# New fronts of the state space layer, and where the fp8 attention rounds its first inputs

## The chip, the cores and the metric

The kernel runs on one core of one Trainium2 chip. A core has five engines that work side by side: TensorE (PE, matrix products into PSUM; its weight loads are counted apart as PEld), VectorE (DVE), ScalarE (ACT), GpSimd (POOL) and SyncE (SP, which here only issues DMAs). Each engine takes its own instructions in order and waits at semaphores for the others. The metric is the device time of one execution in microseconds (us), lower is better.

## The reference

The program is a decoder of four layers with three blocks each, on x of 4 batches x 256 tokens x 256 channels. Every block adds its output to x; all but the last take a layer norm of x as input. The change concerns the tenth block, a state space layer (L3_attn), and its seams with the ninth (a mixture of 8 experts, L2_ffn) and the eleventh (attention with fp8 inputs, L3_xattn).

The state space layer, with 512 inner channels, 16 states and a dt rank of 128:

```python
def _L3_attn_ref(x, W_in, conv_w, conv_b, W_x, W_dt, b_dt, A_log, D, W_out):
    xz = x @ W_in
    xp, z = jnp.split(xz, 2, axis=-1)
    xc = lax.conv_general_dilated(jnp.transpose(xp, (0, 2, 1)), conv_w, (1,), [(1, 1)], feature_group_count=d, ...)
    xc = jax.nn.silu(jnp.transpose(xc + conv_b[None, :, None], (0, 2, 1)))
    x_dbl = xc @ W_x
    dt_in, Bm, Cm = x_dbl[..., :R], x_dbl[..., R:R + S], x_dbl[..., R + S:]
    dt = jax.nn.softplus(dt_in @ W_dt + b_dt)
    A = -jnp.exp(A_log)
    def step(h, ins):
        u_t, dt_t, B_t, C_t = ins
        h = jnp.exp(dt_t[:, :, None] * A) * h + dt_t[:, :, None] * B_t[:, None, :] * u_t[:, :, None]
        return (h, jnp.einsum('bds,bs->bd', h, C_t))
    xsT = (jnp.swapaxes(xc, 0, 1), jnp.swapaxes(dt, 0, 1), jnp.swapaxes(Bm, 0, 1), jnp.swapaxes(Cm, 0, 1))
    _, yT = lax.scan(step, h0, xsT)
    y = (jnp.swapaxes(yT, 0, 1) + xc * D) * jax.nn.silu(z)
    return y @ W_out
```

The convolution runs along the tokens, three taps per channel, one token to each side. The attention behind it normalises x with weights, divides it by four different scales per channel (for q, qx, k and v), and rounds each of the four to bf16 and then to fp8 (e4m3fn) before the products with the weights:

```python
def _div_clamp_fp8(x, scale):
    y = jnp.clip(x.astype(jnp.float32) / scale, -FP8_MAX, FP8_MAX)
    y = y.astype(jnp.bfloat16).astype(jnp.float32)
    return _fp8_roundtrip(y)
```

## The kernel before

x stays in SBUF as 8 tiles of 128 tokens; `k.XNT` holds the normed rows transposed, channels on the partitions. The blocks follow each other; a block's code may also carry pieces of the next one (generators, advanced with `next`), and these pieces are then in the queues among the block's own instructions.

**The mixture of experts** (`l2_ffn`, L1364) leaves the order of its instructions to a scheduler. It loads the state space layer's weights (`l3_loads`, L1415) and carries `l3_ahead` (L1436) in its second half: it multiplies the taps into three copies of the convolution's half of W_in (three DVE products, L1443, with the taps broadcast by three DMAs), norms and turns batches 0 and 1, and computes the front of batch 0.

**A front** (`l3_front`, L1450) is what a batch needs before its scan. PE computes the convolved xp in four tiles of 128 channels with six matmuls each (L1461 to L1465: for the middle tap whole, for the outer taps shifted by a token, two halves of the 256 input channels each), and ACT adds the bias (L1466). PE computes z (L1473), ACT copies it (L1474) and takes the Silu of both (L1476, L1477). PE multiplies by W_x in two banks, one for dt's 128 rows (L1481) and one for B and C (L1486), with an ACT copy each (L1483, L1488); B and C go to DRAM (`bcd`), from where they come back broadcast over the partitions (`bcb`, L83). PE multiplies by W_dt (L1500), and softplus is put together from Abs and Relu (L1504, L1505), Exp (L1507), two DVE operations (L1508, L1509), Ln (L1511) and two POOL operations (L1512, L1514); a third POOL operation, L1516, gives dt times xc (`du`).

**The scan** (`l3_attn`, L1520) has 64 steps g: per batch four chunks c of 128 channels, and in each four groups q of four states. In a step ACT computes the decays of step g+1 into PSUM (`decays`, L1552 four times, L1553), POOL the inputs of step g+2 (`inputs`, L1560), DVE scans step g along the tokens into PSUM (`scan`, L1567, 128 x 1024) and multiplies by C (L1569); PE adds the states of step g-1 up in PSUM with four products by the identity (`sums`, L1579). After each fourth step DVE adds xc times D (`close`, L1586) and POOL multiplies by the Silu of z (L1587). The order on PE, ACT, DVE and POOL is the order of the code here; SP's is scheduled. Tiles come from pools: `unit` has six buffers for inputs and products, `da` two, `h` one, `mm` (the PSUM bank of fronts, turns and outputs) one, `bcb` nine.

Into the steps of batch b are put: one piece per step of the front of batch b+1 (from step 0); from step 10 the norm and turn of batch b+2; at steps 1 and 2 the two output products of batch b-1 with W_out (L1592), each with its addition to x on DVE (L224) right behind; in batches 0 to 2 from step 3 the preparation of the attention's weights (`prepared`: means with ACT, DVE L1854 and L1855, POOL L1857; small scales on DVE, L1872 to L1896; splits into three bf16 parts, ACT L1868 and POOL L1869); in batch 3 from step 4 the norm and turn of the next block's first three batches (`Rows`, L1904; L1928 and L1931 on DVE, L1941 on ACT).

**The fp8 attention** (`l3_xattn`, L1945) starts, in order, with four times scaling (ACT, two products per input, L1988) and rounding (`rounded`, L1990: ACT Abs, then DVE L261, L262, L263, L264) for batch 0, then the scaling for batch 1, then the products of pass 0 (a pass is one batch with one group of heads; 16 passes). The first pass's vectors are normed in two halves: ACT squares (L2043), DVE reduces (L2045) and takes an inverse root by small integer and float steps (L2054 to L2056 and L120 to L129), POOL multiplies (L2059). The rounding of batch 1 is put between them, one input behind each part. Then come turns, scores (PE L2085) with their maximum on DVE (L407), and so on. `early` puts work for later passes into the first ones, among it the scaling and rounding of batches 2 and 3. The routing of the twelfth block (`Routing`, L1664) uses the rounded inputs' memory in passes 14 and 15.

Of the kernel before, what the change touches and what calls it, by code (L numbers as in the profile page):

```python
# [24 lines left out]
P = 128  # L25
# [1389 lines left out]
def l3_loads(k):  # L1415
    nc, a, v = k.nc, k.a, k.nc.vector
    s, s2 = k.wslot(), k.wslot()
    m = k.ssm = {}
    m["win"], m["wx"], m["wdt"] = s.take(2, 1024), s.take(4, 160), s.take(512)
    m["wout"], m["taps"] = s2.take(4, 256), [s2.take(2, 512), s2.take(2, 512)]  # L1420
    k.load(m["win"], rows(a["L3_attn_W_in"]))
    m["soft"] = lambda: k.t([P, 4, S], F32, "soft", 2, k.st)
    soft = [m["soft"]().rearrange("p c t -> p (c t)") for _ in range(2)]
    m["tap"] = [soft[0][:, :512], soft[0][:, 512:], soft[1][:, :512]]
    for i in range(3):
        k.load(m["tap"][i], a["L3_attn_conv_rows"][i : i + 1, :].rearrange("o m -> (o m)").partition_broadcast(P))
    k.load(m["wx"], rows(a["L3_attn_W_x"]))
    k.load(m["wdt"], a["L3_attn_W_dt"])
    k.load(m["wout"], rows(a["L3_attn_W_out"]))
    m["na"] = na = k.t([P, 64], F32, "na", 1, k.st)  # L1430
    nc.scalar.activation(na, k.sm["L3_attn_A_log"], AF.Exp)
    v.tensor_scalar_mul(na, na, -1.0)
    m["ready"] = {}


def l3_ahead(k):  # L1436

    v, m = k.nc.vector, k.ssm


    w = m["win"][:, :, :512]
    for o, i in ((m["taps"][0], 0), (m["taps"][1], 2), (w, 1)):
        v.tensor_tensor(o, w, m["tap"][i].unsqueeze(1).to_broadcast([P, 2, 512]), ALU.mult)  # L1443
        yield
    for b in range(2):
        yield from k.normed_batch(b)
    yield from l3_front(k, 0)


def l3_front(k, b):  # L1450

    nc, v, m = k.nc, k.nc.vector, k.ssm
    win, wx, wdt, taps = (m[n] for n in ("win", "wx", "wdt", "taps"))
    cb, bdt = k.sm["L3_attn_conv_b"], k.sm["L3_attn_b_dt"]
    flat = lambda x: x.rearrange("p c t -> p (c t)")
    h4 = slice(4 * (b % 2), 4 * (b % 2) + 4)
    sz, xc = k.XN[:, h4, :], k.C[:, h4, :]
    part = lambda c, lo, hi: k.XNT[:, c, b * S + lo : b * S + hi]
    for i in range(4):
        o, ms = k.bank()[:, :S], slice(i * P, (i + 1) * P)  # L1460
        nc.tensor.matmul(o, win[:, 0, ms], part(0, 0, S), start=True, stop=False)  # L1461
        for c in range(2):
            nc.tensor.matmul(o[:, 1:], taps[0][:, c, ms], part(c, 0, S - 1), start=False, stop=False)
            nc.tensor.matmul(o[:, : S - 1], taps[1][:, c, ms], part(c, 1, S), start=False, stop=False)
        nc.tensor.matmul(o, win[:, 1, ms], part(1, 0, S), start=False, stop=True)  # L1465
        nc.scalar.activation(xc[:, i, :], o, AF.Identity, bias=cb[:, i : i + 1])  # L1466
        yield
    for i in range(2):
        ps = k.bank()
        for j in range(2):  # L1470
            ms = slice(512 + (2 * i + j) * P, 512 + (2 * i + j + 1) * P)
            for c in range(2):
                nc.tensor.matmul(ps[:, j * S : (j + 1) * S], win[:, c, ms], part(c, 0, S), start=c == 0, stop=c == 1)  # L1473
        nc.scalar.copy(sz[:, 2 * i : 2 * i + 2, :], ps.rearrange("p (c t) -> p c t", c=2))  # L1474
        yield
    nc.scalar.activation(flat(xc), flat(xc), AF.Silu)  # L1476
    nc.scalar.activation(flat(sz), flat(sz), AF.Silu)  # L1477
    yield
    ps = k.bank()
    for c in range(4):  # L1480
        nc.tensor.matmul(ps[:, :S], wx[:, c, 0:P], xc[:, c, :], start=c == 0, stop=c == 3)  # L1481
    dti = k.t([P, S], F32, "dti", 1, k.st)
    nc.scalar.copy(dti, ps[:, :S])  # L1483
    ps = k.bank()
    for c in range(4):
        nc.tensor.matmul(ps[:32, :S], wx[:, c, P:160], xc[:, c, :], start=c == 0, stop=c == 3)  # L1486
    bc = k.t([32, S], F32, "bc", 2, k.st)
    nc.scalar.copy(bc, ps[:32, :S])  # L1488
    bcd = k.t([32, S], F32, "bcd", 2, k.dram)
    k.load(bcd, bc)  # L1490
    yield

    dt, du = (k.t([P, 4, S], F32, n, 2, k.st) for n in ("dt", "du"))
    e, f = m["soft"](), m["soft"]()
    m["ready"][b] = xc, sz, dt, du, bcd
    for i in range(2):
        ps = k.bank()
        for j in range(2):
            c = 2 * i + j
            nc.tensor.matmul(ps[:, j * S : (j + 1) * S], wdt[:, c * P : (c + 1) * P], dti, start=True, stop=True)  # L1500
        for j in range(2):
            c = 2 * i + j
            x = ps[:, j * S : (j + 1) * S]
            nc.scalar.activation(e[:, c, :], x, AF.Abs, bias=bdt[:, c : c + 1])  # L1504
            nc.scalar.activation(dt[:, c, :], x, AF.Relu, bias=bdt[:, c : c + 1])  # L1505
        yield
    nc.scalar.activation(flat(e), flat(e), AF.Exp, scale=-1.0)  # L1507
    v.tensor_scalar_add(flat(f), flat(e), 1.0)  # L1508
    v.scalar_tensor_tensor(flat(e), flat(f), 1.0, flat(e), ALU.subtract, ALU.subtract)  # L1509
    yield  # L1510
    nc.scalar.activation(flat(f), flat(f), AF.Ln)  # L1511
    nc.gpsimd.tensor_tensor(flat(dt), flat(dt), flat(e), ALU.subtract)  # L1512
    yield
    nc.gpsimd.tensor_tensor(flat(dt), flat(dt), flat(f), ALU.add)  # L1514
    yield
    nc.gpsimd.tensor_tensor(flat(du), flat(dt), flat(xc), ALU.mult)  # L1516
    yield


def l3_attn(k):  # L1520
# [15 lines left out]
    bb, cc, das, dbs, hcs, ys, acc = {}, {}, {}, {}, {}, {}, {}  # L1536
# [27 lines left out]
    def scan(g):  # L1564
        b, c, q = at(g)
        h = k.t([P, 4, S], F32, "h", 1, k.ps)
        v.tensor_tensor_scan(flat(h), flat(das.pop(g)), flat(dbs.pop(g)), 0.0, ALU.mult, ALU.add)  # L1567
        hcs[g] = unit()
        v.tensor_tensor(hcs[g], h, cc[b, q], ALU.mult)  # L1569
        if c == 3 and b + 1 < B:  # L1570
            spread(b + 1, q, cc, 16)
# [17 lines left out]
    def output(b, t):  # L1589
        ps = k.bank()  # L1590
        for c in range(4):
            nc.tensor.matmul(ps[:, :D], ys[b][:, c, t * P : (t + 1) * P], wout[:, c, :], start=c == 0, stop=c == 3)  # L1592
        k.add_rows(2 * b + t, ps[:, :D])
# [29 lines left out]
    prep = prepared()  # L1623
# [6 lines left out]
    for b in range(B):  # L1630
        front = l3_front(k, b + 1) if b + 1 < B else of_next_block()
        ahead = rows_ahead(b)
        for i in range(16):
# [4 lines left out]
            if g:  # L1638
                sums(g - 1)
                if i % 4 == 0:  # L1640
                    close(g - 1)
            if b and i in (1, 2):
                output(b - 1, i - 1)
            if b + 1 < B or i >= 4:
                next(front, None)
            if i >= 10:
# [3 lines left out]
        for _ in front:  # L1650
            pass
    for _ in prep:
        pass
    sums(last)
    close(last)
    for t in range(2):
        output(B - 1, t)


PREPARED = {(0, i) for i in range(3, 9)} | {(1, i) for i in range(3, 7)} | {(2, i) for i in range(3, 7)}  # L1660
# [3 lines left out]
class Routing:  # L1664
# [6 lines left out]
    def __init__(self, k, mem, hot):  # L1671
        self.part = {}
        self.k, self.hot = k, hot.rearrange("p (i t e) -> p i t e", i=4, t=2)
        self.xe = [m[:, o : o + ROW] for m in mem for o in (0, 512)]
        self.free = [m[:, o + ROW : o + 512] for m in mem for o in (0, 512)]
# [196 lines left out]
def l3_scales(k):  # L1872
# [28 lines left out]
    k.l3 = dict(ws=ws, ws2=ws2, lnw=lnw, ism=ism, psc=psc, iin=iin)  # L1901
# [43 lines left out]
def l3_xattn(k):  # L1945
# [16 lines left out]
    ins = {n: k.t([P, 2, B * S], BF16, "in_" + n, 1) for n in ("q", "qx", "k", "v")}  # L1962
# [12 lines left out]
    spare = k.XN.rearrange("p t d -> p (t d)")  # L1975
    r32, r16s = spare[:, 1024:1536], [spare[:, o : o + 256].bitcast(BF16) for o in (1536, 1792)]
# [6 lines left out]

    def scaled(b, n):

        bs = slice(b * S, (b + 1) * S)
        for c in range(2):
            nc.scalar.mul(ins[n][:, c, bs], k.XNT[:, c, bs], iin[n][:, c : c + 1])  # L1988

    def rounded(b, n):  # L1990
        x, m = ins[n][:, :, b * S : (b + 1) * S], next16(0)
        two = lambda y: y.rearrange("p (c s) -> p c s", c=2)
        k.to_e4m3fn_ahead(two(m), x)
        k.bf16_to_e4m3fn(x, x, two(m), two(r32), below=True)
# [5 lines left out]
    class Pass:  # L2000
# [15 lines left out]
        def thrice(self, ps, t, n):  # L2016
            for c in range(2):
                for i in range(3):
                    nc.tensor.matmul(ps, ins[n][:, c, self.tokens(t)], self.w[n][i][:, c, :],  # L2019
# [132 lines left out]
    routing = Routing(k, [ins[n].rearrange("p c s -> p (c s)").bitcast(F32) for n in IN], spare[:, 1792:2048])  # L2152
# [20 lines left out]
    def early(n, i):  # L2173

        if n == 0 and i == 0:
# [17 lines left out]
    for n in IN:  # L2193
        scaled(0, n)
        rounded(0, n)
    for n in IN:
        scaled(1, n)
    now, last = Pass(0), None
    for i, steps in enumerate(PARTS[:4]):
# [3 lines left out]
        rounded(1, IN[i])  # L2203
# [345 lines left out]
def _spread(w, groups, heads, dh, stride=32):  # L2549
# [10 lines left out]
    "L0_attn_bq": 16, "L0_attn_bk": 4, "L1_xattn_bq": 4, "L1_xattn_bk": 4, "L3_attn_conv_b": 4, "L3_attn_b_dt": 4,  # L2560
# [9 lines left out]
def layout(i):  # L2570
# [37 lines left out]
    o["L3_attn_conv_rows"] = i["L3_attn_conv_w"].reshape(-1, 3).T  # L2608
# [44 lines left out]
```

## Time and profile before

| | us |
|---|---|
| median of three runs | 2325.26 (2324.23 to 2329.4) |
| profiled execution, its own time | 2324.57 |
| span, first to last instruction | 2322.6 |
| first scan starts | 1134.01 |
| last product by C (L1569) ends | 1450.35 |
| first maximum of scores (L407 of pass 0) starts | 1489.61 |

Over the whole span PE is busy for 81% of the time, DVE for 64%, ACT 49%, POOL 33%, and the granted clock of TensorE is 0.924 on average. Those shares mix twelve blocks of different kinds. For this change the 316 us between the first scan and the last product matter, with some 40 us on either side, so the profile is read by stretches of time: how busy each engine was in a stretch, what each engine waited for there, and which single instructions stand before and behind a wait. "L1567 <- POOL unit L1560" in a list of waits means: line 1567's instruction waited, and the last thing to come was the tile `unit`, written by POOL in line 1560.

### The profile page before, as it was taken

Reading aid. Unit: us, or ns where it says so; the run is one execution under the profiler, and the core shown is the slowest. Engines: PE = TensorE matmul, PEld = TensorE weight load, DVE = VectorE, ACT = ScalarE, POOL = GpSimd, SP = SyncE. Lnnn points to the kernel's source line nnn. Section 1 sums busy time; section 2 is a strip of 40 time slices with the busy share of each in tenths; the row PEclk is TensorE's granted clock in tenths of the full one; section 3 lists DMA queues with packets and bytes.
Section 4 is the critical chain, followed back from the end, with each engine's and each line's share of the span. In section 5 each row is a group of like instructions: output and inputs, shape, how many; then the busy total and the mean of one; then the engine's idle time right before and its main releaser. Section 6 shows DMA issues by size and latency. Waiting matters only on the chain. (4 is left out here: it accounts for less than half of the span.)

```text
span 2322.6 us, 31804 instructions
## 1 busy us (share of the span) xinstructions
PE 1891.4 (81%) x11396; PEld 1313.3 (57%) x11396; DVE 1486.7 (64%) x3539; ACT 1128.3 (49%) x2581; POOL 757.3 (33%) x621
## 2 busy tenths in 40 slices
PE   7889997897887589896668765778999999998794
PEld 4566564454443344563546643556777777777583
DVE  6654637634656844547587889777566666657765
ACT  2321322333334533334666564666767767675252
POOL 2221210001000100003566673244456356444544
PEclk9999997999988799997879898889999999999897
DMA  4000008000700620000320120101001000003295
GB/s 172 1 1 28 1 32 267 1 1 15 229 29 1 214 76 1 2 24 1 109 69 23 55 91 0 37 19 37 1 19 37 1 19 14 1 2 108 99 327 186
DMA packets 88899, 136.49 MB, mean 59 GB/s; under 512 B 5281, under 2 KB 69026, under 8 KB 88482
## 3 DMA queue, kind: packets, MB, share of 16 engines
q1 hardware_dynamic: 84754, 123.59, 16.2%
q0 software_dynamic: 3840, 10.75, 1.2%
q8 instruction: 91, 1.49, 0.3%
q14 instruction: 70, 0.57, 0.1%
q10 hardware_dynamic: 144, 0.08, 0.1%
HBM read 82.31 MB, written 52.10 MB: 58 GB/s over the span
## 5 line engine op out<-in xcount | busy, mean ns | idle before, releaser
L417 ACT ACTIVATE prob<-mm,smx 128x256 f32<-128x256 f32 x392 | 183.8, 477 | 254.8 <-DVE smx L407 229.2
L616 DVE TENSOR_REDUCE mt<-pair 128x2 f32<-128x512 f32 (+1 forms) x256 | 133.5, 586 | 179.3 <-PE pair L609 179.2
L1579 PE MATMUL acc<-unit,c 128*128 128x256 f32 x512 | 149.0, 442 | 100.8 <-DVE unit L1569 85.8
L2093 POOL TENSOR_TENSOR prob<-prob,sinv 128x512 f32<-128x512 f32 x128 | 139.5, 1095 | 185.3 <-DVE sinv L2092 159.7
L407 DVE TENSOR_REDUCE smx<-mm 128x2 f32<-128x512 f32 x196 | 134.3, 686 | 94.1 <-PE mm L2085 69.6
L1579 PEld LDWEIGHTS acc<-unit,c 128*128 128x128 f32 x512 | 107.3, 218 | 137.3 <-DVE unit L1569 102.1
L648 ACT ACTIVATE pt<-pair 128x768 f32<-128x768 f32 (+1 forms) x128 | 103.7, 862 | 147.2 <-PE pair L642 147.2
L1567 DVE TENSOR_TENSOR_SCAN h<-da,unit 128x1024 f32<-128x1024 f32 x64 | 146.8, 2294 | 30.5 <-POOL unit L1560 13.5
L426 POOL TENSOR_TENSOR prob<-prob,sinv 128x512 f32<-128x512 f32 x68 | 75.5, 1112 | 242.2 <-DVE sinv L552 177.0
L1560 POOL TENSOR_TENSOR unit<-du,bcb 128x1024 f32<-128x1024 f32 x64 | 149.4, 2356 | 6.8 <-DVE h L1567 3.7
L1552 ACT ACTIVATE da<-dt,na 128x256 f32<-128x256 f32 x256 | 122.6, 479 | 58.5 <-DVE h L1567 49.6
L560 PE MATMUL acc<-pt,c 128*128 128x256 f32 x512 | 134.9, 387 | 3.7 <-ACT pt L2104 3.6
L2059 POOL TENSOR_TENSOR x<-x,hrs 128x1536 f32<-128x1536 f32 x32 | 87.6, 2757 | 117.0 <-DVE hrs L2056 117.0
L231 POOL TENSOR_TENSOR c<-c,w 128x256 f32<-128x256 f32 x24 | 16.9, 729 | 321.0 <-ACT fqq L323 163.0
L2112 DVE TENSOR_SCALAR c<-acc,ism 128x256 bf16<-128x256 f32 x128 | 61.2, 479 | 82.1 <-PE acc L560 82.1
L2101 PE MATMUL tr<-c,prob 128*128 128x128 f32 x512 | 82.3, 286 | 30.1 <-POOL prob L2093 23.0
L560 PEld LDWEIGHTS acc<-pt,c 128*128 128x128 f32 x512 | 94.2, 196 | 17.8 <-ACT pt L2104 4.7
L2072 PE MATMUL tr<-c,x 128*128 128x128 f32 x384 | 60.6, 291 | 43.1 <-ACT pt L2104 20.6
L2101 PEld LDWEIGHTS tr<-c,prob 128*128 128x128 f32 x512 | 63.3, 147 | 55.4 <-POOL prob L2093 34.3
L596 PE MATMUL pair<-c,c 128*128 128x256 bf16 x384 | 69.2, 276 | 24.3 <-DVE mt L616 14.0
L2104 ACT COPY pt<-tr 128x512 f32<-128x512 f32 x128 | 76.4, 598 | 16.4 <-PE tr L2101 16.4
L2129 PEld LDWEIGHTS <-cat 128*128 128x128 bf16 x768 | 75.5, 98 | 12.8
(629 smaller groups left out, 4842.2 us busy)
## 6 DMA issues: line engine op xcount, KB each, us to landing
xs<-zero SPq DMA_DIRECT2D x3, 13056.0 KB
bcb<-bcd SPq DMA_DIRECT2D x32, 512.0 KB, 4.2
we<-in_L_ffn_w_dram SPq DMA_DIRECT2D x33, 384.0 KB, 5.0
wa<-in_L_ffn_w_dram SPq DMA_DIRECT2D x15, 384.0 KB, 4.0
xr<-xs SPq DMA_DIRECT2D x8, 544.0 KB, 6.1
w<-in_L_xattn_wproj_dram SPq DMA_DIRECT2D x8, 512.0 KB, 7.2
xr<-ys SPq DMA_DIRECT2D x6, 512.0 KB, 4.8
w<-in_L_xattn_wq_dram SPq DMA_DIRECT2D x5, 512.0 KB, 4.1
```

Of the source, the lines that this page charges most:

```text
L407: nc.vector.tensor_reduce(mx, sc, AX.X, ALU.max, negate=True)
L417: nc.scalar.activation(pr[:, t, :w], sc[:, t, :w], AF.Exp, bias=mx[:, t : t + 1], scale=scale, accum_out=sums[:, t : t + 1],)
L560: k.nc.tensor.matmul(ob[:, :S], v[:, c, :], pt[:, c, :], start=c == 0, stop=c == 1)
L616: nc.vector.tensor_reduce(c, pr[p][:, :, t, :w], AX.X, ALU.max, negate=True)
L648: nc.scalar.activation(o, st[p][:, :, : S + w1], AF.Exp)
L1552: nc.scalar.activation(da[:, i, :], ready[b][2][:, c, :], AF.Exp, scale=na[:, col : col + 1])
L1560: nc.gpsimd.tensor_tensor(dbs[g], ready[b][3][:, c : c + 1, :].to_broadcast([P, 4, S]), bb[b, q], ALU.mult)
L1567: v.tensor_tensor_scan(flat(h), flat(das.pop(g)), flat(dbs.pop(g)), 0.0, ALU.mult, ALU.add)
L1579: nc.tensor.matmul(acc[b, c][:, :S], k.identf, hc[:, i, :], start=q == 0 and i == 0, stop=q == 3 and i == 3)
L2059: nc.gpsimd.tensor_tensor(x, x, rs[:, t, :].unsqueeze(2).to_broadcast([P, 12, P]), ALU.mult)
L2093: nc.gpsimd.tensor_tensor(d["pr"], d["pr"], ri.unsqueeze(2).to_broadcast([P, 2, S]), ALU.mult)
L2101: nc.tensor.transpose(tb[:, c * S + t * P : c * S + (t + 1) * P], pr[:, t, c * P : (c + 1) * P], k.identf)
```

## The change

The fronts. The convolution is no longer in W_in: PE computes xp plainly with two matmuls per tile, and ACT makes three tiles of it, xc = tap 1 times xp plus bias, e = tap 0 times xp, f = tap 2 times xp; two POOL additions add e and f to xc, shifted by a token. The tap products, copies and DMAs in the mixture of experts go. Both W_x products lie in one bank. With `hold` (batches 1 to 3) a matmul is put into one step and what reads it into the next; a front starts two steps ahead of the batch before its own (at step 14), has 15 pieces and leaves out step 2. Without it (batch 0) softplus' last operations and `du` are on DVE in place of POOL.

The scan. The two output products stay at steps 1 and 2, their additions move between scan and product of steps 2 and 3. The norm and turn of batch b+2 move to steps 6, 7, 8, 9 and 11. The preparation of the attention's weights moves to batch 2, steps 11 and 13 to 15, and batch 3, steps 0 to 9.

The attention's start. Batch 0's four inputs get a tile of their own (`ins0`), and are scaled and rounded at the end of the scan's block: one behind the last sums, two between the last output products and their additions, one behind. Batch 1's are scaled behind the norms of pass 0, where q and qx are also rounded; k and v are rounded in the first two steps of pass 0. The scratch tiles and the routing's memory move accordingly.

```diff
-    w = m["win"][:, :, :512]
-    for o, i in ((m["taps"][0], 0), (m["taps"][1], 2), (w, 1)):
-        v.tensor_tensor(o, w, m["tap"][i].unsqueeze(1).to_broadcast([P, 2, 512]), ALU.mult)
-        yield
...
-    yield from l3_front(k, 0)
+    yield from l3_front(k, 0, False)
...
+    def product(o, i):
+        for c in range(2):
+            nc.tensor.matmul(o, win[:, c, i * P : (i + 1) * P], k.XNT[:, c, bs], start=c == 0, stop=c == 1)
     for i in range(4):
-        o, ms = k.bank()[:, :S], slice(i * P, (i + 1) * P)
-        nc.tensor.matmul(o, win[:, 0, ms], part(0, 0, S), start=True, stop=False)
-        for c in range(2):
-            nc.tensor.matmul(o[:, 1:], taps[0][:, c, ms], part(c, 0, S - 1), start=False, stop=False)
-            nc.tensor.matmul(o[:, : S - 1], taps[1][:, c, ms], part(c, 1, S), start=False, stop=False)
-        nc.tensor.matmul(o, win[:, 1, ms], part(1, 0, S), start=False, stop=True)
-        nc.scalar.activation(xc[:, i, :], o, AF.Identity, bias=cb[:, i : i + 1])
-        yield
+        o = k.bank()[:, :S]
+        product(o, i)
+        if hold:
+            yield
+        w = lambda j: cw[:, 3 * i + j : 3 * i + j + 1]
+        nc.scalar.activation(xc[:, i, :], o, AF.Identity, bias=cb[:, i : i + 1], scale=w(1))
+        nc.scalar.mul(e[:, i, :], o, w(0))
+        nc.scalar.mul(f[:, i, :], o, w(2))
+        if not hold or i == 2:
+            yield
     for i in range(2):
         ps = k.bank()
...
+        if i == 0:
+            nc.gpsimd.tensor_tensor(xc[:, :, 1:], xc[:, :, 1:], e[:, :, : S - 1], ALU.add)
+        else:
+            nc.gpsimd.tensor_tensor(xc[:, :, : S - 1], xc[:, :, : S - 1], f[:, :, 1:], ALU.add)
+        if hold:
+            yield
...
+    for c in range(4):
+        nc.tensor.matmul(ps[:32, S:], wx[:, c, P:160], xc[:, c, :], start=c == 0, stop=c == 3)
+    yield
     dti = k.t([P, S], F32, "dti", 1, k.st)
     nc.scalar.copy(dti, ps[:, :S])
...
+    last = nc.gpsimd if hold else v
+    last.tensor_tensor(flat(dt), flat(dt), flat(e), ALU.subtract)
     yield
     nc.scalar.activation(flat(f), flat(f), AF.Ln)
-    nc.gpsimd.tensor_tensor(flat(dt), flat(dt), flat(e), ALU.subtract)
+    last.tensor_tensor(flat(dt), flat(dt), flat(f), ALU.add)
     yield
-    nc.gpsimd.tensor_tensor(flat(dt), flat(dt), flat(f), ALU.add)
-    yield
-    nc.gpsimd.tensor_tensor(flat(du), flat(dt), flat(xc), ALU.mult)
+    last.tensor_tensor(flat(du), flat(dt), flat(xc), ALU.mult)
     yield
...
         v.tensor_tensor_scan(flat(h), flat(das.pop(g)), flat(dbs.pop(g)), 0.0, ALU.mult, ALU.add)
+        if b and g % 16 in (2, 3):
+            add(b - 1, g % 16 - 2)
         hcs[g] = unit()
...
+            if b + 1 == B and i >= 4 or b + 1 < B and i < 14 and (b == 0 or i != 2):
+                next(front, None)
+            if (b, i) == (0, 3):
+                next(front)
             if b and i in (1, 2):
                 output(b - 1, i - 1)
-            if b + 1 < B or i >= 4:
-                next(front, None)
-            if i >= 10:
+            if b + 2 < B and i >= 14:
+                if i == 14:
+                    front = l3_front(k, b + 2)
+                next(front)
+            if i in AHEAD:
                 next(ahead, None)
...
+    def input_of_next(i):
+        x = k.l3["ins0"][:, i]
+        l3_scaled(k, x, 0, ("q", "qx", "k", "v")[i])
+        l3_rounded(k, x, m16[i % 2], t32)
+
     sums(last)
+    input_of_next(0)
     close(last)
     for t in range(2):
         output(B - 1, t)
-PREPARED = {(0, i) for i in range(3, 9)} | {(1, i) for i in range(3, 7)} | {(2, i) for i in range(3, 7)}
+        input_of_next(t + 1)
+        add(B - 1, t)
+    input_of_next(3)
+AHEAD = 6, 7, 8, 9, 11
+PREPARED = {(2, 11), (2, 13), (2, 14), (2, 15)} | {(3, i) for i in range(10)}
...
     def early(n, i):
+        if n == 0 and i < 2:
+            rounded(1, IN[i + 2])
...
-    for n in IN:
-        scaled(0, n)
-        rounded(0, n)
-    for n in IN:
-        scaled(1, n)
     now, last = Pass(0), None
     for i, steps in enumerate(PARTS[:4]):
         for st in steps:
             front(now, st)
         flush()
-        rounded(1, IN[i])
+    for n in IN:
+        scaled(1, n)
+        if n in ("q", "qx"):
+            rounded(1, n)
```

## The prediction

> **What bounds the kernel now.** I read the page first, then the stages in time, then each engine's waits, then single steps. The chain that ended last says nothing of this stage: none of its pieces lies between 1100 and 1500 us. The span is 2322.6 us, its execution took 2324.57 us (2 us lie around the span), 0.69 below the median of three runs, 2325.26. Sums go against 2324.57.
>
> Busy time by stretch (columns: stretch, its length, busy time of PE, weight load, DVE, ACT and POOL with counts, granted clock, DMA share, GB/s). The first row ends where the first scan starts, the next four are the scans of batches 0 to 3, the last is the start of the fp8 attention:
> ```profile
> 1092.00:1134.00 42.00, 28.09 (x123) 20.02 (x121) 10.49 (x20) 24.50 (x46) 15.41 (x13) 0.83 0.43 151
> 1134.00:1209.50 75.50, 49.80 (x176) 38.40 (x177) 63.64 (x82) 45.83 (x96) 43.49 (x27) 0.82 0.09 30
> 1209.50:1291.40 81.90, 61.82 (x237) 46.79 (x237) 64.17 (x59) 52.31 (x109) 55.38 (x28) 0.85 0.15 52
> 1291.40:1372.00 80.60, 62.11 (x248) 47.55 (x247) 65.22 (x44) 52.83 (x114) 55.47 (x29) 0.92 0.21 71
> 1372.00:1450.40 78.40, 45.43 (x168) 33.54 (x166) 73.10 (x73) 36.92 (x88) 42.89 (x22) 0.87 0.06 21
> 1450.40:1489.60 39.20, 25.61 (x117) 17.53 (x118) 28.87 (x69) 22.44 (x46) 6.35 (x3) 0.83 0.17 54
> ```
> DVE is the fullest engine in every batch, and yet idles 17 us and 15 us in batches 1 and 2. Undisturbed, a step is one scan and one product:
> ```profile
> 1209.49 2.28 DVE L1567 TENSOR_TENSOR_SCAN h<-da,unit 128x1024 f32<-128x1024 f32 x1
> 1211.81 1.23 DVE L1569 TENSOR_TENSOR unit<-h,bcb 128x1024 f32<-128x1024 f32 x1
> 1213.17 2.30 DVE L1567 TENSOR_TENSOR_SCAN h<-da,unit 128x1024 f32<-128x1024 f32 x1
> ```
> That is 3.69 us per step, 236 us for 64. What DVE waited for from 1134 to 1450.4, and two of ACT's waits (us in all, times, longest):
> ```profile
> DVE h L1567 <- POOL unit L1560: 13.5, 3, 9.8
> DVE h L1567 <- ACT da L1553: 12.5, 9, 3.9
> DVE c L224 <- PE mm L1592: 9.1, 5, 2.9
> DVE y L1586 <- PE acc L1579: 6.7, 3, 3.3
> DVE wmean L1854 <- ACT w L1848: 6.5, 2, 3.5
> DVE soft L1508 <- ACT soft L1507: 1.9, 2, 1.0
> ...
> ACT c L1466 <- PE mm L1465: 35.6, 11, 5.4
> ACT bc L1488 <- PE mm L1486: 9.2, 3, 3.7
> ```
> (The 9.8 lies before the first scan.) ACT stands behind PE's convolution 35.6 us in all, and the decays of the next step stand behind ACT: that makes the 12.5. One more loss wears the dress of work:
> ```profile
> 1181.70 5.39 DVE L1880 TENSOR_SCALAR ws<-ws,c 128x4 f32<-128x4 f32 x3
> ```
> Three tiny instructions take 5.39 us while POOL runs L1587 and two L1560 from 1181.72 to 1187.07; so does a 128x6 L1928 at 1410.03 (2.25 us) inside a POOL instruction of 1409.90 to 1412.25.
>
> **Part 1, the first front, up to the first scan.** Convolution before: four tiles of six matmuls at 2.58 us (1093.3 to 1106.2, partly cold), one ACT bias each. After: two matmuls (0.86), three ACT instructions (0.47 each, pitch 0.36, so 1.1) per tile, then two POOL additions at about 2.35 (nearest: L1514, same size). ACT and PE overlap over tiles: about 5, plus 4.7 of POOL, of which the first addition lies beside the z products; about 2 us won. The W_x products take one bank and no longer wait for ACT's dti copy; 1 us. Behind the logarithm's input, POOL's three instructions (1124.37 to 1131.55) become three on DVE at 1.22: the first two are beside the table load and logarithm as before, so the chain from Ln's end (1125.3) to du goes from 6.25 to 2.45; 3.8. DVE loses three tap products of 1.22 in the mixture of experts, where DVE idles; a little over 1 at most. First scan about 1126, 8 us earlier. What comes late next: the broadcast rows. In this stretch DMA moves 6.33 MB from 1116 to 1133, near 400 GB/s. Afterwards six weight loads (2 MB, some 5.5 us) stand on SP's queue between the first two broadcasts and the other six. If the weights' slot opens as early as before, the second B row lands near 1128 and the second scan loses 2. I take 6; bounds 3 (broadcasts late for every step) and 10.
>
> **Part 2, the 64 steps.** DVE's own work without any wait: 64 x 3.69 = 236.2; 16 closes at 0.17 net 2.6; six output additions at 0.42, 2.5; softplus pairs 3 x 1.95, 5.9; statistics and norms of batches 2 and 3, 3.8 each, 7.6; the next block's, 7.5; weight means 4.7; scales 1.84. Sum 268.8. The stage took 316.35 (1134.0 to 1450.35), so 47.5 is waiting: 42.2 listed, 5.4 of stretched instructions. The change takes nothing from the 268.8. Of the waits:
> - ACT's decays 12.5 -> 5. Every product now gets a whole step before ACT reads it, so the 35.6 go; ACT gains 8 instructions a batch (2.9 us) against 14 us or more of room. Left is the step with both Silu: decays 2.2, two tables at 1.28, two Silu at 1.06 make 6.9, against 3.69 plus the 2.8 that the second decay buffer leaves.
> - PE's output 9.1 -> 0: the addition now stands a step later, behind a scan of 2.3. PE's sums 6.7 -> 2: they stood behind 2.58 us of convolution, now behind 0.86; the last close stays (2.09, with part 3).
> - Softplus 1.9 -> 0 (Exp is a step ahead). POOL 5.0 -> 4.5: start-up and the third of a weight. Weight means 6.5 -> 5: moved to batches 2 and 3, with ACT as busy.
> - Stretched instructions 5.4 -> 9. POOL gets two additions per batch, 3 x 4.7 = 14.1 on 197.2, in a shorter stage: busy 72% instead of 62%. In proportion 6.3; if each of some 18 bursts of small DVE instructions met POOL in mid-instruction (72% x half of 2.36), 15. I take 9, nearer to the measured one.
>
> Left 25.5; stage 294.3, gain 22. Bounds: no wait left but 8, 40; and waits that merely change name, 10. POOL has room: 16 x 2.36 + 5 x 2.35 + 4 x 0.73 = 52.4 per batch against DVE's 65 to 68, and an input may be 6 us late before a scan sees it. The weights' preparation moves to the end of batch 2 and to batch 3, where POOL has 42.9 of 78.4 busy and loses no front; it ends at step 9 of batch 3, 25 us ahead of its use. The normed rows of the batch after next move to steps 6 to 11; their transposes are PE's. SP carries the same broadcasts, each still three steps ahead.
>
> The Trainium skill, "SBUF — State Buffer", section "SBUF: two separate sides", says that VectorE and GpSimd share a port pair under an exclusive lock: an instruction of GpSimd, or a VectorE one with two SBUF inputs or in a two-port mode, holds it throughout and the other is fully blocked. The 5.39 and 2.25 us agree, and the rule speaks against a change that fills POOL; by it every one of those bursts pays, and the stage would be some 6 to 33 us longer than above.
>
> **Part 3, the start of the fp8 attention.** Before, from the last product E = 1450.35: DVE waits 2.09, 1.59 and 2.09 for PE, then rounds four inputs (1457.37 to 1464.8, 1.86 each); the first product starts at E+9.1; batch 1's roundings stand between the first norms' reductions, one stretched by POOL (2.53 and 3.12 us instead of 0.28 and 0.69). First score maximum at E+39.26. After, three of the four roundings fill those waits: products from about E+7 (2 won), and the norms come forward by the 1.9 and 4.1 of the q and qx roundings and part of the stretch: maximum at about E+29.2, 10 won. But batch 1's k and v are now rounded inside pass 0, on DVE ahead of the reductions for the next scores: 2 x 1.86 plus waits for ACT's Abs (0.63) and the two scalings (0.90) give back about 5.3. Net 4.7; bounds 0 and 9. Batch 0's inputs lying elsewhere, and the routing memory's new places, cost nothing: their readers end long before pass 14.
>
> **Sum:** 6 + 22 + 4.7 = 32.7; 2324.57 - 32.7 = 2291.9, I say 2292.
>
> **Rivals.** (a) Port bound: each of the 18 bursts waits for a whole POOL instruction or two; 18 x 2.36 = 42 in place of 9 at the worst, at the likeliest double to triple, 15 to 25. For it: 5.39 us for three instructions, and POOL at 72%. Against: mean L1560 is 2.356 throughout, and in 316 us only 5.4 were lost. Time 2292 + 6 to 16: about 2303.
> (b) DVE at its floor: scans run at 3.69 from start to end, with some 10 us of waits. For it: 1209 to 1220 and most of batch 3 run so. Against: the Silu step. Time 2292 - 15: about 2276.
> (c) Slower: the TensorE clock falls. PE was busy 219.2 in the stage at granted 0.82 to 0.92, 190 at full; without 3 x 6.9 of convolution 169. Fewer matmuls leave longer idle gaps; at half clock PE needs 339, becomes the bound, and the time is 2324.57 + 22.7 - 10.7 = 2337. It decides once PE needs over 316.35 + 10.7 = 327, at a mean granted clock below 169/327, 0.52. For it: 0.59 in 1278 to 1290, where PE was busy 5.27 of 12. Against: 1434 to 1450, sums alone, 8.41 of 16 busy, was granted 1.00. "TensorE: Matmul & The Clock Gate" of the Trainium skill, Part 1, says that an idle window brings half clock and a busy one full; by that the gaps decide, not the load.
> (d) The change only renames waits: with one PSUM bank for the fronts, the held matmul waits until ACT has read, and the sums behind it. Silu and Ln steps lag 3.2 and 2.1 us, over three fronts 16; 2308. It is no more than that, since ACT's other steps (3.3) are below 3.69.
>
> **Chances.** Forecast 0.45, (a) 0.17, (b) 0.17, (d) 0.09; the clock or another thing that takes all, 0.12 (of which within 0.2%, about what a measurement can tell from no change, 0.03). Faster 0.88, same 0.03, slower 0.09. Range: the low end takes 10 + 40 + 8 = 58 won, 2266; the high end 3 + 10 + 0 = 13 won, 2311; it leaves out (c) and little else.
>
> **What the profile after would show.** First scan near 1128 or earlier, L1519 and L1521 on DVE; ACT's wait for the convolution gone from its list; no DVE wait for output L1599; close waits short; 64 scans from first to last product in about 294 us; POOL near 72%; the first score maximum 29 us behind the last product, and roundings behind it. Wrong if the scan waits for POOL's inputs in the middle of a batch (POOL or the lock binds), if broadcasts land behind the scans of steps 1 to 3, if PE's clock is at one half in the steps, or if DVE instructions of a few elements take over 2 us again and again.

## The result and the profile after

The changed kernel takes 2303.45 us (median of four runs, 2298.62 to 2304.6) against 2324.74 for the kernel before; the ratio is 0.9903 with a 95% interval of 0.9881 to 0.9925. It is faster by 21 us, where 32.7 were forecast. The profiled execution took 2303.11 us, with a span of 2301.0, 21.6 below that of before.

Of the three places that the prediction priced, the 64 steps gave more than forecast, the attention's start about as much, and the stretch up to the first scan little more than half; together they won 36 us, and a fourth place gave 16 back. The span's difference by stretches, each bounded by the same instruction in both traces:

| stretch | before | after | won | forecast |
|---|---|---|---|---|
| start to ACT's copy L188, ahead of all that was changed but the loads of the taps (from 1018.9 before) | 1026.79 | 1024.86 | 1.9 | 0 |
| from there to the first scan | 107.22 | 103.75 | 3.5 | 6 |
| first scan to the last product by C | 316.34 | 287.92 | 28.4 | 22 |
| last product to the routing's last send (end of POOL's last `xs` DMA issue) | 754.21 | 750.09 | 4.1 | 4.7 |
| last send to the first turn of the last block on PE | 6.42 | 15.35 | -8.9 | 0 |
| from there to the end | 111.62 | 119.00 | -7.4 | 0 |

The 64 steps first. Busy time by stretch of the kernel after, with the columns of the prediction: up to the first scan, the four batches, and up to the first maximum of scores:
```profile
1080.00:1128.60 48.60, 27.92 (x98) 16.47 (x100) 20.82 (x57) 29.32 (x57) 15.49 (x16) 0.68 0.30 98
1128.60:1196.10 67.50, 49.05 (x185) 36.66 (x185) 65.12 (x55) 53.08 (x116) 50.52 (x25) 0.89 0.22 80
1196.10:1264.20 68.10, 51.95 (x205) 38.28 (x205) 65.92 (x58) 52.11 (x114) 51.24 (x26) 0.95 0.19 62
1264.20:1335.60 71.40, 52.82 (x197) 38.52 (x198) 67.46 (x52) 55.25 (x120) 58.50 (x33) 0.90 0.24 81
1335.60:1416.50 80.90, 44.57 (x152) 33.18 (x151) 77.93 (x91) 41.39 (x92) 49.36 (x29) 0.81 0.00 0
1416.50:1446.10 29.60, 23.12 (x116) 16.17 (x118) 24.49 (x63) 19.30 (x38) 6.34 (x3) 0.94 0.22 71
```
DVE is now busy for 276.4 of 287.9 us: batches 1 and 2, which idled 17 and 15 us, idle 2 and 4. All that it waited for from the first scan to the last product (the 2.5 lie before the first scan):
```profile
DVE h L1572 <- POOL unit L1565: 2.8, 3, 2.5
DVE h L1572 <- ACT da L1558: 2.4, 2, 2.2
DVE c L224 <- PE mm L1599: 0.3, 1, 0.3
```
Of the 42 us of listed waits before, 3 are left. What DVE loses now is in its busy time. From its timeline, the attention's small scales at the start of batch 3 and the inverse root of the next block's norm:
```profile
1343.11 4.12 DVE L1913 TENSOR_SCALAR ws<-ws,c 128x4 f32<-128x4 f32 x3
1347.27 2.27 DVE L1915 TENSOR_TENSOR ws<-ws 128x12 f32<-128x12 f32 x1
1349.58 0.17 DVE L1916 TENSOR_SCALAR ws<-ws 128x12 f32<-128x12 f32 x1
...
1373.58 2.28 DVE L120 TENSOR_SCALAR ra_x<-rf 128x6 f32<-128x6 f32 x1
1375.89 1.07 DVE L124 TENSOR_SCALAR ra_h<-ra_x 128x6 int32<-128x6 int32 x1
1377.00 2.26 DVE L125 TENSOR_SCALAR ra_y<-ra_h 128x6 int32<-128x6 int32 x1
```
and POOL at the first of the two places:
```profile
1340.35 4.67 POOL L1565 TENSOR_TENSOR unit<-du,bcb 128x1024 f32<-128x1024 f32 x2
1345.09 2.12 POOL L1902 TENSOR_TENSOR w<-w,wq 128x1024 f32<-128x1024 f32 x1
1347.17 2.34 POOL L1565 TENSOR_TENSOR unit<-du,bcb 128x1024 f32<-128x1024 f32 x1
```
L1913 ends at 1347.23, just behind POOL's 1345.09 to 1347.21, and L1915 at 1349.54, just behind the 1347.17 to 1349.51 that followed: a few elements per partition, and each time a whole POOL instruction goes by first. Over the stage such stretches add up to 19 us (7 before).

The stretch up to the first scan next. From the copy that ends batch 0's turn (L188), with which the first front can begin, to the Silu of `xc`, before:
```profile
1092.39 0.59 ACT L188 COPY c<-tr 128x512 f32<-128x512 f32 x1 [0.29 <-PE tr L187]
...
1106.91 1.06 ACT L1476 ACTIVATE c<-c 128x1024 f32<-128x1024 f32 x1
```
and after, with the two POOL additions that now stand between:
```profile
1086.34 0.58 ACT L188 COPY c<-tr 128x512 f32<-128x512 f32 x1 [0.29 <-PE tr L187]
...
1104.23 1.06 ACT L1482 ACTIVATE c<-c 128x1024 f32<-128x1024 f32 x1 [2.29 <-POOL c L1476]
```
```profile
1099.79 2.35 POOL L1474 TENSOR_TENSOR c<-c,soft 128x1020 f32<-128x1020 f32 x1
1102.21 1.99 POOL L1476 TENSOR_TENSOR c<-c,soft 128x1020 f32<-128x1020 f32 x1
```
From the end of the copy to the Silu it takes 13.9 us before and 17.3 after: the new convolution is slower here. From the same copy to the first scan the two kernels take 41.0 and 41.7 us, so the 3.5 us of the table were won ahead of the front, between the first copy L188 of the table and this one (66.2 us before, 62.1 after).

Then the loss. The chain that ended last, around the change from the eleventh to the twelfth block (start, us, what; SPq is SP's sequencer):
```profile
2154.45 0.97 POOL xs L1845
2155.42 0.20 POOL in_k L1837
...
2155.77 0.09 POOL in_k L1837
2155.86 0.16 POOL in_k L1838
2156.02 0.04 POOL in_k L1839
2156.06 0.20 SPq L83
...
2162.22 10.32 DMA we<-in_L_ffn_w_dram
...
2172.64 9.28 DMA xr<-xs
2181.97 0.70 PE tr L2480 x2
```
Before the change, this chain ran from POOL's sends to `xr<-xs` (3.98 us) and to PE, without SP or weights in it. The twelfth block gathers its rows (`xr`) with DMAs on SP's queue, behind its first nineteen weight loads, five `wa` and fourteen `we`. SP's timeline before:
```profile
2093.19 20.29 SPq L83 DMA_DIRECT2D wa<-in_L_ffn_w_dram  x5
2113.58 45.17 SPq L83 DMA_DIRECT2D we<-in_L_ffn_w_dram  x14
2206.95 1.48 SPq L83 DMA_DIRECT2D xr<-xs  x3
```
and after:
```profile
2052.20 105.49 SPq L83 DMA_DIRECT2D wa<-in_L_ffn_w_dram  x5
2158.11 13.78 SPq L83 DMA_DIRECT2D we<-in_L_ffn_w_dram  x14
2172.64 3.76 SPq L83 DMA_DIRECT2D xr<-xs  x3
```
The first `wa` load goes out early, the second not before 2156. The program says what it waits for: the routing's first eight POOL DMAs, DVE, PE, ACT and POOL, where the kernel before waited for DVE, PE and POOL. The addresses say why. The buffers of `wa` end at byte 129248 of a partition; before, the routing's memory (the input tiles) began at 129984; after, `ins0` lies at 128672 to 132768. The 576 bytes in common belong to the input q, which nobody reads after pass 12 (in e1, where q has a tile of its own, its last read is near 1929), but they are one tile with the part that the routing uses, and the wait is for the whole tile. Its last reader is POOL's L1837, which copies token numbers for the last batch (2155.71 to 2155.90).

### The profile page after: what moved, and what is told of

The parts are those of the page before. It is cut to its first block, busy times and chain, and to the rows that moved or that the text cites. A ratio compares the mean times of both kernels' runs of the same rounds, so it can differ in the third digit from the quotient of the medians.

```text
span 2301.0 us, 31538 instructions
## 1 busy us (share of the span) xinstructions
PE 1860.2 (81%) x11232; PEld 1285.1 (56%) x11268; DVE 1498.3 (65%) x3539; ACT 1137.9 (49%) x2613; POOL 765.8 (33%) x626
## 3 DMA queue, kind: packets, MB, share of 16 engines
q1 hardware_dynamic: 84322, 122.80, 16.3%
## 5 line engine op out<-in xcount | busy, mean ns | idle before, releaser
L407 DVE TENSOR_REDUCE smx<-mm 128x2 f32<-128x512 f32 x196 | 134.1, 685 | 86.1 <-PE mm L2134 64.6
L1557 ACT ACTIVATE da<-dt,na 128x256 f32<-128x256 f32 x256 | 122.3, 478 | 71.3 <-DVE h L1572 61.6
```

The lines of the kernel that those rows point to most:

```text
L407: nc.vector.tensor_reduce(mx, sc, AX.X, ALU.max, negate=True)
L1557: nc.scalar.activation(da[:, i, :], ready[b][2][:, c, :], AF.Exp, scale=na[:, col : col + 1])
```

## Experiments

Theory: the three parts together win about what was forecast, and the overlap takes some 16 us back. Rival for the loss: the loads come late because the passes and the routing run closer together, whatever the memory. For the 28 us of the scan two rivals as well: the order with held reads, or the smaller load on PE. Times of the kernel before drift between sets (2318 to 2325), so ratios are compared, and stages from the traces.

**e1, the tile split.** The same addresses, two tiles:
```diff
-    ins0 = k.t([P, 4, 2, S], BF16, "ins0", 1, k.late)
+    ins0 = k.t([P, 2, S], BF16, "ins0q", 1, k.late), k.t([P, 3, 2, S], BF16, "ins0", 1, k.late)
...
-    words.append(ins0.rearrange("p i c s -> p (i c s)").bitcast(F32)[:, 256:])
+    words.append(ins0[1].rearrange("p i c s -> p (i c s)").bitcast(F32))
```


> The changed kernel, but batch 0's four inputs lie in two tiles, q alone (1024 bytes per partition) and the other three, at the same addresses. The first weight buffers of the last block (wa) overlap 576 bytes of the first tile only. Theory overlap (the wait of these loads for the last reader of the one big tile, the copy of the token numbers at 2155.9, takes 16.3 us back): the nineteen loads go out before 2120, the first gathered rows arrive some 6 us behind the last send as before the change, and the time is 2303.5 - 16 = 2287 (2284 to 2291), ratio to the kernel before about 0.984. Rival collision (the loads come late because pass 15 and the routing run closer together, whatever the memory): no change, 2303 +- 4.

Measured: 2290.09 us, ratio 0.9858 (0.9837 to 0.9878). That is 13.4 below the changed kernel's median of another set, and 10.5 by the two ratios. SP's timeline:
```profile
2051.67 8.49 SPq L83 DMA_DIRECT2D wa<-in_L_ffn_w_dram  x5
2060.26 59.22 SPq L83 DMA_DIRECT2D we<-in_L_ffn_w_dram  x14
2167.57 2.20 SPq L83 DMA_DIRECT2D xr<-xs  x3
```
The nineteen loads are out by 2120, the rows follow the last send as they did before (6.16 us to PE's first turn, 6.42 before), and the end follows after 113.7. The rival falls: only one tile was made two. Against its set's kernel before, the gain is 2322.79 - 2290.09 = 32.7 us.

**e2, the same overlap in the kernel before.** One declaration changes place:
```diff
+    ins = {n: k.t([P, 2, B * S], BF16, "in_" + n, 1) for n in ("q", "qx", "k", "v")}
     for tag, n in (("ssq", 24), ("hrs", 24), ...):
         k.t([P, 2, 12] if tag in ("ssq", "hrs") else [P, n], F32, tag, 2)
-    ins = {n: k.t([P, 2, B * S], BF16, "in_" + n, 1) for n in ("q", "qx", "k", "v")}
```


> The kernel before, with one thing changed: the four input tiles of the fp8 attention are allocated ahead of its small tiles, so that the last wa buffer overlaps the first of them, which the routing uses to its end. Nothing else moves. Theory overlap: the nineteen loads, which went out from 2093 to 2158, wait until the routing's last copy near 2194 and take about as long as in the changed kernel; 2325 + 16 = 2341 (2336 to 2346). Rival collision: 2325 +- 4, since the passes stand as they stood.

Measured: 2334.77, ratio 1.0047 (1.0030 to 1.0064), 12 us slower by the medians and 11 by the ratio, a little less than the range expected. SP's timeline:
```profile
2089.48 102.22 SPq L83 DMA_DIRECT2D wa<-in_L_ffn_w_dram  x5
2191.80 15.85 SPq L83 DMA_DIRECT2D we<-in_L_ffn_w_dram  x14
2208.38 3.57 SPq L83 DMA_DIRECT2D xr<-xs  x3
```
The same picture in a kernel whose passes were not touched; its 64 steps take 316.35 again. From the last send to PE's first turn 16.36 instead of 6.42, and 118.3 to the end. The price in time, 11 to 12 here and 10.5 to 13.4 by e1, lies below the 16 of the two profiles. Up to PE's first turn it is clear: 15.35 and 16.36 us with the overlap, 6.2 to 7.8 in the eleven kernels without it. Behind that turn it is not: 119.0 and 118.3 with the overlap, but 111.6 to 118.1 without.

**e3, held reads undone.** As e1, each matmul and its readers in one step again:
```diff
         product(o, i)
-        if hold:
-            yield
         w = lambda j: cw[:, 3 * i + j : 3 * i + j + 1]
...
-        if not hold or i == 2:
-            yield
+        yield
...
     for c in range(4):
         nc.tensor.matmul(ps[:32, S:], ...)
-    yield
```


> As e1, but in the fronts of batches 1 to 3 each matmul and the ACT instructions that read it stand in the same step again (15 pieces as before, the additions on POOL kept, everything else kept). Theory order (the stage was shortened mainly because ACT no longer waits for PE in the middle of a step): ACT's waits for L1455, L1487 and L1504 come back, with them DVE's waits for the decays, some 10 to 20 us: 2297 to 2307. Rival load (the shorter convolution on PE did it, 0.86 instead of 2.58 us per tile, and the order little): 2287 to 2291.

Measured: 2299.07, ratio 0.9891 (0.9869 to 0.9913); the 64 steps 293.8 (e1: 288.7). DVE's wait for the decays and ACT's for the fronts' products come back:
```profile
DVE h L1566 <- ACT da L1552: 10.1, 8, 3.1
...
ACT c L1474 <- PE mm L1455: 12.4, 4, 4.8
ACT c L1462 <- PE mm L1455: 10.9, 9, 4.4
```
The mechanism is as the order theory has it, its share by itself only 5 of the 28 us.

**e4, the small scales off DVE.**
```diff
-    v.memset(ws, 1.0)
+    g, act = k.nc.gpsimd, k.nc.scalar
+    g.memset(ws, 1.0)
     for n, lo, hi in (("q", 0, 4), ("qx", 4, 8), ("k", 8, 10)):
-        v.tensor_scalar_mul(ws[:, lo:hi], ws[:, lo:hi], sm["w" + n + "_scale"])
+        for c in range(lo, hi):
+            act.copy(ws[:, c : c + 1], sm["w" + n + "_scale"])
...
-    v.tensor_mul(ws2, ws, ws)
-    v.tensor_scalar_mul(ws2, ws2, 1.0 / P)
+    g.tensor_tensor(ws2, ws, ws, ALU.mult)
+    act.mul(ws2, ws2, 1.0 / P)
```
(`lnw` goes to ACT, `psc` to POOL in the same way.)

> As e1, but the small scales of the attention (l3_scales: ws, ws2, lnw, psc; 13 small DVE instructions) are made by ACT and POOL; the five reciprocals stay on DVE. In the changed kernel the first four of these took 4.12 + 2.27 us on DVE beside POOL's inputs, where 0.3 to 0.5 would do. Theory port (DVE is the floor of the 64 steps, and its short instructions lose whole POOL instructions): 5.9 us of stretch and 1.3 us of work go, unless the first reciprocal runs into POOL in their place; 64 steps in 281 to 285 us instead of 288, time 3 to 7 below e1. Rival (the stretch is hidden elsewhere, DVE is not the floor): same as e1 within 1.

Measured: the 64 steps 282.65, 6.1 below e1. DVE's busy time in them falls by 6.2 (276.7 to 270.5), so time on DVE costs the stage one for one. In DVE's timeline scan now follows product almost at once:
```profile
1340.49 1.23 DVE L1576 TENSOR_TENSOR unit<-h,bcb 128x1024 f32<-128x1024 f32 x1
1341.63 0.34 DVE L1925 RECIPROCAL ism<-c 128x32 f32<-128x32 f32 x1
...
1342.10 2.28 DVE L1572 TENSOR_TENSOR_SCAN h<-da,unit 128x1024 f32<-128x1024 f32 x1
```
The time, 2288.48, ratio 0.9848 (0.9830 to 0.9867), is the lowest ratio of all, but only 1.6 below e1, where 3 to 7 were expected, and not clear of it: its last block took 115.9 from the first turn, e1's 113.7.

**e5, the convolution back on PE**, with held reads: `l3_loads` and `l3_ahead` make the tap copies as before, and in the front
```diff
-        product(o, i)
+        nc.tensor.matmul(o, win[:, 0, ms], part(0, 0, S), start=True, stop=False)
+        for c in range(2):
+            nc.tensor.matmul(o[:, 1:], m["taps"][0][:, c, ms], part(c, 0, S - 1), start=False, stop=False)
+            nc.tensor.matmul(o[:, : S - 1], m["taps"][1][:, c, ms], part(c, 1, S), start=False, stop=False)
+        nc.tensor.matmul(o, win[:, 1, ms], part(1, 0, S), start=False, stop=True)
         if hold:
             yield
...
-            nc.gpsimd.tensor_tensor(xc[:, :, 1:], xc[:, :, 1:], e[:, :, : S - 1], ALU.add)
```


> As e1, with the convolution as before the change: three tap copies of W_in, six matmuls per tile on PE, one ACT bias, no additions on POOL; the new order with held reads stays. The 64 steps took 288.7 us in e1 and 316.3 before. Theory order (a held matmul is covered whether it takes 0.86 or 2.58 us): 287 to 292 us, and a little less stretch on DVE, since POOL loses 14 us. Rival load (2.58 us of matmuls ahead of the sums make DVE wait for the sums and close late): 295 to 303 us.

Measured: the 64 steps 286.3, the time 2286.65, ratio 0.9855 (0.9831 to 0.9879), the same as e1. A held matmul is covered at either length, and without the additions on POOL the stretches on DVE fall by some 5 us. In the scan, then, the new convolution by itself gains nothing, and in the first front it costs: from the copy of batch 0's turn to the first scan e5 takes 38.9 us, the eight kernels with the new convolution 40.3 to 41.7. What is longer in e5 lies ahead of that copy, where DVE's products of the taps with W_in are back: 71.3 us from the first copy L188, in those eight 62.0 to 64.6.

**e9, both undone at once** (e3's and e5's edits together):

> As e1, with both undone at once: the convolution on PE with six matmuls per tile (as e5, 286.3 us for the 64 steps) and each matmul read in its own step (as e3, 293.8). Theory either-is-enough (DVE's waits come from ACT standing behind a long matmul; a short matmul or a held read removes most of them alone): 300 us or more, a jump far above the sum of the two. Rival additive (each has its own small share, and the rest of the 28 us came from the earlier front, the preparation's new place and the later additions together): 288.7 + 5.1 - 2.4 = 291 +- 3.

Measured: the 64 steps 301.3, the time 2306.21, ratio 0.9928 (0.9899 to 0.9957). Alone the two cost 5.1 and -2.4, together 12.5: either one covers most of the wait of the other. ACT's wait for the convolution, and DVE's for the decays:
```profile
DVE h L1573 <- ACT da L1559: 13.3, 13, 3.1
...
ACT c L1475 <- PE mm L1474: 27.5, 11, 5.9
ACT c L1481 <- PE mm L1464: 12.4, 4, 4.8
```

**e7 and e8, the scan's other moves undone one at a time.** e7 puts each output addition behind its product again, e8 the weights' preparation into batches 0 to 2:
```diff
-        if b and g % 16 in (2, 3):
-            add(b - 1, g % 16 - 2)
...
                 output(b - 1, i - 1)
+                add(b - 1, i - 1)
```
```diff
-PREPARED = {(2, 11), (2, 13), (2, 14), (2, 15)} | {(3, i) for i in range(10)}
+PREPARED = {(0, i) for i in range(3, 9)} | {(1, i) for i in range(3, 7)} | {(2, i) for i in range(3, 7)}
```


> As e1, but the additions of the output products stand right behind them again, in steps 1 and 2, where DVE waits for PE. By the list of waits before (9.1 us in five waits in the stage, 2.9 at most): six waits of 1.5 to 2.9, the 64 steps 9 to 12 us longer than e1's 288.7. Rival (with the shorter convolution PE is ready in time): 2 us or less.

> As e1, but the preparation of the attention's weights stands in the steps of batches 0 to 2 again, where the fronts are. By the list of waits before, weight means 6.5 us, POOL 1.3, and more for the decays, because ACT and POOL now carry front and weights in the same steps: the 64 steps 5 to 12 us longer than e1's 288.7. Rival (only the place differs): within 3 us.

Measured: 288.9 us for the 64 steps in both, as in e1; 2289.22 (ratio 0.9866) and 2290.35 (0.9871). Neither of the two losses that were expected came. In e7 DVE does wait for the output product again (3.7 us in all, 2.8 at most), but its stretches are 3 us fewer.

**e10, all four undone** (e9, e7 and e8 together):

> As e9, and also the output additions right behind their products (e7) and the weights' preparation in batches 0 to 2 (e8): of the scan's changes only the earlier front of batches 2 and 3, the norms' new steps and the joint W_x bank are left. If these four are where the 28 us came from, the 64 steps take 312 to 318 us again; what is missing to 316.3 belongs to the earlier front and the W_x bank.

Measured: 307.7 us for the 64 steps, below the 312 to 318 expected; 2314.56, ratio 0.9971 (0.9955 to 0.9987). The output additions and the preparation, free by themselves, cost 6.5 when the fronts are slow as well. Of the 27.6 us between e1 and the kernel before, the four make 19.0; 8.6 are left for the earlier front, the norms' steps and the joint bank of W_x, which were not separated.

**e6 and e11, the attention's start undone.** e6 rounds batch 0's inputs in the attention's own code, as the kernel before does:

> As e1, with the start of the fp8 attention as before: batch 0's inputs rounded after the last output addition, batch 1's between the first norms. The step of the prediction: first score maximum again about 39 us behind the last product instead of 30.4, of which the later passes gain back a part, since k and v of batch 1 are no longer in pass 0: 4 to 6 us over e1 at the end, 2294 to 2296. Rival (all is regained inside pass 0): within 2 us of e1.

Measured: 2297.58, ratio 0.9901 (0.9881 to 0.9921), but it did not give the old order: with `ins0` free early, the roundings went between the last scans, and the 64 steps took 299.4. So it says nothing on the start. e11 fixes the order:
```diff
     sums(last)
-    input_of_next(0)
     close(last)
     for t in range(2):
         output(B - 1, t)
-        input_of_next(t + 1)
         add(B - 1, t)
-    input_of_next(3)
+    for i in range(4):
+        input_of_next(i)
...
     for i, steps in enumerate(PARTS[:4]):
         for st in steps:
             front(now, st)
         flush()
+        rounded(1, IN[i])
```


> As e1, with the four roundings of batch 0 behind the last output addition and batch 1's between the first norms, as before the change, but in a fixed order (in e6 the roundings of batch 0 went between the last scans). First score maximum 38 to 40 us behind the last product (e1: 30.4); measured from the first scan to the last send, 4 to 6.5 us more than e1's 1041.0.

Measured: 2299.61, ratio 0.9899 (0.9871 to 0.9928). The first maximum of scores stands 38.2 behind the last product (e1: 30.4), and the last send 756.7 (e1: 752.3): 7.8 us won at the first scores, of which 4.4 are left at the last send. From first scan to last send it is 1044.6 against 1041.0, 3.6, a little under what was expected. The times of e11 and e1 lie 9.5 us apart; in their profiles 6.5 us of the difference stand ahead of the first scan and 2.8 in the last block, where the edit changes nothing. The stretch from last product to last send has its own variation: in the nine kernels with the new start it takes 749.6 to 752.3.

## Why the prediction was right, and where it was not

- **The step that failed** is the last sentence of part 3: that batch 0's inputs lying elsewhere and the routing memory's new places cost nothing, since their readers end long before pass 14. The readers of the inputs do (near 1929 in e1); but the routing's own readers go on to 2156, and half of the question was who is to be written over them next. That was the twelfth block's weights, and the wait goes by tile. Forecast 0, in the profile 16.3, by e1 and e2 10.5 to 13.4. No rival had it, and no bound of the range stands for it: that the time stayed inside is luck. So is that 2303.45 falls on rival (a)'s 2303, which put the loss into the steps. With the tile split the gain is 32.7, the sum forecast, but that too is a coincidence of the total. In e1's profile, whose span is 36.8 below that of before, the steps won 27.6, the stretch from the first copy L188 to the first scan 4.5 and the attention's start 2.0; the other 2.7 lie in stretches that were not changed.
- **The 64 steps**: 28.4 won where 22 were forecast, from two sizes that were off in opposite directions. Waits: 16.5 were left standing (decays 5, weight means 5, POOL 4.5, sums 2), and 3 are. Stretches: 9 were taken, and it is 19, which is rival (a)'s size; 7 were there before by the same count, not 5.4. So the sign that the prediction gave for being wrong, tiny DVE instructions of over 2 us again and again, did appear (six times), and the steps still gained more than forecast. The 287.9 us less 3 and 19 leave 266 for DVE's own work, some 3 less than the 268.8 of the sum. POOL's share of busy time, forecast 72%, is 209.6 of 287.9, 73%. The Trainium skill, "SBUF — State Buffer", section "SBUF: two separate sides", says of the port pair that VectorE and GpSimd share that the loser is blocked for the other's whole instruction; 4.12 and 2.27 us for a few elements, ending within 0.03 us of POOL's instructions, agree, and e4 shows the price.
- **The forecast reason for the stage**, ACT standing behind PE's convolution, is right as a mechanism (e3, e9). That held reads alone remove it was not asked in the prediction; e5 and e3 show that either half does most of it.
- **The output's and the weights' preparation's waits**, 9.1 and 1.5 in the sum, are no separate gains: e7 and e8 cost nothing alone.
- **The first front** is a second step that failed, behind a number that came out within its bounds: 3.5 in the profiled pair, where 6 were forecast. The convolution was to give 2 us and took 3.4: from the copy of batch 0's turn to the Silu it takes 13.9 us before and 17.3 after. PE's and ACT's part took 12.5, with work of the experts in between, where about 5 were put, and the two POOL additions follow with 4.4, behind nearly all of the z products, where the first was to lie beside them. Another 1.6 went between W_dt's first product and the logarithm. W_x in one bank won 0.8 (forecast 1), DVE in POOL's place 3.5 (forecast 3.8), and in sum the front is no shorter (41.0 us before, 41.7 after). The 4.1 that were won ahead of it were put at "a little over 1 at most". In all profiles this stretch takes 62.0 to 64.6 us in the eight kernels without the tap products and 66.2 to 71.3 in the five with them. The three products are 3.7 us of DVE's time; how they lengthen it was not separated. From the first copy L188 to the first scan it is 102.8 to 106.0 against 106.2 to 110.7, so 3.5 is little more than what a profile varies by. The broadcast rows, for which 2 us were set aside, were not late: behind the 2.46 us before the first scan, POOL's inputs cost DVE 0.3 us in all the steps. The rate read for them, 6.33 MB near 400 GB/s, is 6.14 MB and 361 GB/s in the trace.
- **The attention's start**: first scores 29.55 us behind the last product, forecast 29.2; at the last send 4.1 are left, forecast 4.7; e11 against e1 says 4.4. That is not far above the 2.7 us by which this stretch varies between kernels with the same start.
- **Rivals**: (c) the clock did not fall (0.81 to 0.95 in the four batches). (b), DVE at its floor, is what the stage looks like, with the losses of (a) inside it. (d) did not happen.

## What to carry to other kernels

When a tile changes its place, look not only at its readers but at what is allocated over it next: a load that waits for the last byte's reader holds up everything behind it on its queue, and it is seen only in the next block. A shared byte is enough where waits go by tile, and a second tile boundary at the right address costs nothing. Where several changes remove the same wait, undo them together before calling any of them useless: one alone may show no loss while the other covers it.

## What was not expected of the hardware

- A short DVE instruction among long POOL ones costs more than the mean of a random meeting. The prediction counted 18 bursts of small DVE instructions; the trace has 11. Four of them lost next to nothing, five 1.1 to 2.6 us, and two 5 to 6 us. That is 1.7 us for a burst, where POOL's 73% of half an instruction of 2.36 us would be 0.9. One burst lost twice in a row (4.12 and 2.27 us for four instructions); POOL's next instruction starts there within 0.1 us of the end of its last.
- The last block, from its first turn to its end, takes 111.6 to 118.1 us in the eleven kernels whose code there is the same and whose loads are early (111.6 before and in e7, 118.1 in e10). What sets this is open; it hides a difference like e4's 6 us, and part of the 7.4 us that the profiled pair lost there may be of this kind.
